# First pages of three experts loaded ahead of the page table, with page buffers in memory of their own

## The chip, the cores and the metric

The kernel runs on one core of a Trainium2 chip. The metric is the device time in microseconds of one execution, the median of several timed runs. Beside it there is one profiled execution, whose page and trace are quoted below. The engines are called as in the profile: PE is the matmul engine, PEld its weight loads, DVE the vector engine, ACT the scalar engine, POOL the general engine, which here issues the indexed transfers, and SP the engine that issues most plain transfers.

## The reference

Two layers work on 128 graphs of 64 nodes with 256 features, 8192 rows in all. Layer 0 is a graph stage and a mixture over 64 experts, layer 1 a graph stage and a mixture over 8 experts. Only the end of layer 1 matters for the change (cut):

```python
# --- layer 1 ---
x = x + _L1_gnn_ref(_layernorm(x), adj, ...)          # the graph stage
x = x + _L1_ffn_ref(_layernorm(x), ...)

def _L1_ffn_ref(x, Wg, bg, bias, W1, b1, W2, b2):     # 8 experts, 256 -> 512 -> 256
    x_flat = x.reshape(-1, D_MODEL)
    gate_logits = x_flat @ Wg + bg + bias
    topk_vals, topk_idx = jax.lax.top_k(gate_logits, 2)
    topk_w = jax.nn.softmax(topk_vals, axis=-1)
    combine = (jax.nn.one_hot(topk_idx, 8) * topk_w[..., None]).sum(axis=1)
    h = jax.nn.relu(jnp.einsum('td,edh->teh', x_flat, W1) + b1)
    y = jnp.einsum('teh,ehd->ted', h, W2) + b2
    return jnp.einsum('ted,te->td', y, combine).reshape(x.shape)
```

Each row goes to 2 of 8 experts, and which ones is known only when its logits are.

## The kernel before

It has four large stages, one after the other: layer 0's graph stage in 32 blocks of 256 rows, layer 0's experts, a block stage (the end of layer 0, layer 1's graph stage and its routing, again 32 blocks), and layer 1's experts. In the block stage each normalized row is scattered, with its two routing values, into a table in main memory that has a region per expert. For that the kernel keeps the running end of each region (`run`), counts a block's rows per expert on PE, works out the places on DVE, and sends the rows with four indexed transfers from POOL:

```python
# in class Router
    def places(self, b, hot):
        # ... the places of the block's rows from the counts in PSUM and the running ends ...

    def send(self, row, xs):
        for t in range(self.T):
            for k in range(self.K):
                i = self.nc.gpsimd.indirect_dma_start(
                    out=self.table[:, :], out_offset=bass.IndirectOffsetOnAxis(ap=row[:, t, k:k + 1], axis=0),
                    in_=xs[:, t, k, :], in_offset=None)
                self.alone(i.ins, "send")

    def fill(self, engine, row):
        i = engine.dma_start(
            out=self.table[ds(row, self.pg), :].rearrange("(t p) d -> p t d", p=P),
            in_=self.filler)
        self.alone(i.ins, "fill", "send", "full")
```

`alone` tells the framework which transfers touch different rows, so that they need not wait for each other. When all blocks are sent, `page_table` turns the counts into pages of 256 rows: first the full pages of all experts, then the partial ones. It leaves, for each page, its first row in the table and its expert (`tab`), which engines read into registers:

```python
        v.tensor_scalar(full, cnt, 1.0 / pg, (pg - 1.0) / (2 * pg), op0=ALU.mult, op1=ALU.subtract)
        v.tensor_scalar(full, full, MAGIC, None, op0=ALU.add)
        v.tensor_scalar(full, full, -MAGIC, None, op0=ALU.add)
        v.scalar_tensor_tensor(part, full, -float(pg), cnt, op0=ALU.mult, op1=ALU.add)
        v.tensor_scalar(part, part, 0.0, None, op0=ALU.is_gt)
        v.tensor_tensor_scan(cum, num, self.zero, 0.0, op0=ALU.add, op1=ALU.add)
        # ... start row and expert of each page into self.tab ...

    def load(self, what, i, engine):

        top = (self.spare, self.E - 1)[what]
        _, v = self.nc.values_load_multi_w_load_instructions(
            self.tab[i // 4:i // 4 + 1, what, :], engines=[engine], min_val=0, max_val=top,
            skip_runtime_bounds_check_because="the page table holds no other values for any counts")
        return v
# ...
    def fetch(self, i, row, out):
        d = self.nc.sync.dma_start(out=out, in_=self.table[ds(row, self.pg), :].rearrange("(t p) d -> p t d", p=P))
        if i < self.full_pages:
            self.tc.declare_no_dep(d.ins, group=self.name + "fill", reason="full pages have no filler rows")
            self.tc.add_to_no_dep_group(self.name + "full", d.ins)
```

The stages of a block or page are staggered: the pairs are a lag and a function, and the order of the pairs is the order of each engine's instructions for PE, DVE and ACT, which is kept as written. The order on the queues of SP and POOL is the framework's.

```python
        def place1(b):
            B = blocks[b]
            r1.send(r1.places(b, B["hot"]), B["xs"])

        staggered(NB, (
            (-2, load3),
            # ...
            (3, choose1),
            # ...
            (3, count1),
            # ...
            (3, place1),
            (0, layer_out_c),
            (4, load_w2),
        ))
        r1.page_table(work.tile([P, 512], F32, name="scratch", bufs=1))

    with tc.tile_pool(name="wx1", bufs=2) as wx, \
            tc.tile_pool(name="pt4", bufs=2, space=PSUM) as pt_pool, \
            tc.tile_pool(name="ph4", bufs=4, space=PSUM) as ph_pool, \
            tc.tile_pool(name="py4", bufs=2, space=PSUM) as py_pool:
        PG = 2 * P
        pages = [dict() for _ in range(r1.pages)]
        regs = {}

        def fetch1(i):
            Q = pages[i]
            if i % 4 == 0 or i == r1.likely_pages:
                regs["row"], regs["esp"] = r1.load(0, i, ENG.SP), r1.load(1, i, ENG.SP)
            row, e = regs["row"][i % 4], regs["esp"][i % 4]
            Q["x"] = x = wx.tile([P, 2, W], F32, name="px", bufs=4)
            r1.fetch(i, row, x)
            Q["w"] = w = wx.tile([P, F1W], F32, name="pw", bufs=3)
            nc.sync.dma_start(out=w, in_=fw1[ds(e, 1)].rearrange("o p f -> p (o f)"))
            Q["b2"] = b2 = wx.tile([P, D], F32, name="pb2", bufs=4)
            nc.sync.dma_start(out=b2, in_=a["L1_ffn_b2"][ds(e, 1), :].to_broadcast([P, D]))

        def flip1(i):
            Q = pages[i]
            pt = pt_pool.tile([P, KD, PG], F32, name="pt")
            ops.transpose(pt, Q["x"])
            Q["xT"] = xT = wx.tile([P, KD, PG], F32, name="pxT")
            nc.scalar.copy(xT, pt)

        # up(i): 16 products with Q["w"], relu on ACT
        # down(i): 16 products with fw2[expert], bias and weight on DVE, two adding scatters from POOL

        stages = (-2, fetch1), (0, flip1), (1, down), (0, up)
        staggered(r1.likely_pages, stages)
        with tc.If(r1.needed(r1.likely_pages)):
            staggered(r1.pages, stages, r1.likely_pages)
```

`likely_pages` is 69 here; pages beyond that run only if the routing needs them. The page pool `wx` is opened after the pools of the block stage are closed, so its buffers lie where the block stage's tiles lay. A constant row that is added by a matmul is split into bf16 parts, and stored twice side by side, by `row_parts`:

```python
    def row_parts(rest, name):

        part = small.tile([P, D], BF16, name="part", bufs=1)
        out = const.tile([P, 2, D], BF16, name="p_" + name)
        for i in range(3):
            nc.vector.tensor_copy(part, rest)
            nc.vector.tensor_sub(rest, rest, part)
            if i == 0:
                nc.vector.tensor_scalar(out[:, 0, :], part, ident[:, 0:1], None, op0=ALU.mult)
            else:
                nc.vector.scalar_tensor_tensor(out[:, 0, :], part, ident[:, i:i + 1], out[:, 0, :],
                                               op0=ALU.mult, op1=ALU.add)
        nc.vector.tensor_copy(out[:, 1, :], out[:, 0, :])
        return out

```

Of the kernel before, what the change touches and what calls it, by code (L numbers as in the profile page):

```python
# [78 lines left out]
class Router:  # L79
# [15 lines left out]
    def __init__(self, tc, pool, small, dram, n, D, E, K, T, pg, S, epoch, name, total=None):  # L95
# [46 lines left out]
        self.table = dram.tile([self.spare + pg, self.W], F32, name=name + "x")  # L142
        self.fill(nc.sync, self.spare)

# [21 lines left out]
    def fill(self, engine, row):  # L166
        i = engine.dma_start(
            out=self.table[ds(row, self.pg), :].rearrange("(t p) d -> p t d", p=P),
            in_=self.filler)
        self.alone(i.ins, "fill", "send", "full")  # L170
# [113 lines left out]
    def send(self, row, xs):  # L284
        for t in range(self.T):
            for k in range(self.K):
                i = self.nc.gpsimd.indirect_dma_start(  # L287
                    out=self.table[:, :], out_offset=bass.IndirectOffsetOnAxis(ap=row[:, t, k:k + 1], axis=0),
                    in_=xs[:, t, k, :], in_offset=None)
                self.alone(i.ins, "send")  # L290
# [18 lines left out]
    def page_table(self, scratch):  # L309
# [29 lines left out]
        v.tensor_scalar(part, part, 0.0, None, op0=ALU.is_gt)  # L339
        v.tensor_tensor_scan(cum, num, self.zero, 0.0, op0=ALU.add, op1=ALU.add)  # L340
# [48 lines left out]
    def needed(self, n):  # L389

        _, (v,) = self.nc.values_load_multi_w_load_instructions(
            self.total_pages[0:1, :], min_val=0, max_val=self.pages,
            skip_runtime_bounds_check_because="these pages hold any routing")
        return v > n

# [16 lines left out]
def two_layer_gnn_moe_kernel(ctx: ExitStack, tc: tile.TileContext, a: dict, out: bass.AP):  # L412
# [49 lines left out]
    def row_parts(rest, name):  # L462

        part = small.tile([P, D], BF16, name="part", bufs=1)
        out = const.tile([P, 2, D], BF16, name="p_" + name)
        for i in range(3):
            nc.vector.tensor_copy(part, rest)
            nc.vector.tensor_sub(rest, rest, part)
            if i == 0:
                nc.vector.tensor_scalar(out[:, 0, :], part, ident[:, 0:1], None, op0=ALU.mult)  # L470
            else:
                nc.vector.scalar_tensor_tensor(out[:, 0, :], part, ident[:, i:i + 1], out[:, 0, :],
                                               op0=ALU.mult, op1=ALU.add)
        nc.vector.tensor_copy(out[:, 1, :], out[:, 0, :])
        return out
# [316 lines left out]
    fw2 = keep.tile([P, E1, KF, D], F32, name="fw2")  # L792
    with tc.tile_pool(name="c3", bufs=1) as c3, \
# [18 lines left out]
        pg = pmix.tile([P, T, E1], F32, name="pg")  # L812
        r1.begin(counts, work, pmix.tile([P, 2, T, E1], F32, name="pos"))
# [154 lines left out]
        def place1(b):  # L968
            B = blocks[b]
            r1.send(r1.places(b, B["hot"]), B["xs"])  # L970

# [24 lines left out]
    with tc.tile_pool(name="wx1", bufs=2) as wx, \  # L996
            tc.tile_pool(name="pt4", bufs=2, space=PSUM) as pt_pool, \
# [3 lines left out]
        pages = [dict() for _ in range(r1.pages)]  # L1001
        regs = {}

        def fetch1(i):
            Q = pages[i]
            if i % 4 == 0 or i == r1.likely_pages:
                regs["row"], regs["esp"] = r1.load(0, i, ENG.SP), r1.load(1, i, ENG.SP)
            row, e = regs["row"][i % 4], regs["esp"][i % 4]
            Q["x"] = x = wx.tile([P, 2, W], F32, name="px", bufs=4)
            r1.fetch(i, row, x)  # L1010
# [3 lines left out]
            nc.sync.dma_start(out=b2, in_=a["L1_ffn_b2"][ds(e, 1), :].to_broadcast([P, D]))  # L1014

# [18 lines left out]
        def down(i):  # L1034
            Q = pages[i]
            if i < E1:
                r1.fill_end(i)
            if i % 4 == 0 or i == r1.likely_pages:
                regs["e"] = r1.load(1, i, ENG.PE)

# [6 lines left out]
            for t in range(2):  # L1047
                for c in range(KF):
                    nc.tensor.matmul(py[:, t, :], lhsT=Q["hid"][:, c, ts(t, P)],  # L1049
                                     rhs=fw2[:, ds(regs["e"][i % 4], 1), c, :].rearrange("p o d -> p (o d)"),  # L1050
# [7 lines left out]
        staggered(r1.likely_pages, stages)  # L1058
        with tc.If(r1.needed(r1.likely_pages)):
            staggered(r1.pages, stages, r1.likely_pages)  # L1060
# [32 lines left out]
```

## Time and profile before

| what | value |
|---|---|
| timed runs | 2144.85 us median of 3 (2144.35 to 2147.32) |
| span of the profiled execution | 2446.3 us |
| PE, PEld busy | 2036.7 us (83%), 1744.9 us (71%) |
| DVE, ACT, POOL busy | 1186.3 us (48%), 1013.6 us (41%), 1157.1 us (47%) |
| moved by transfers | 398.93 MB, mean 163 GB/s |
| mean granted PE clock | 0.931 |

The profiled execution is longer than a timed one, so a length in the trace is not yet a length in the metric. The page cuts the span into 40 slices of 61 us. Each digit is the busy share of a slice in tenths, and PEclk is the clock granted to PE in tenths of full speed:

```profile
PE   7888888888884578877878886888888699999998
DVE  5777776776666322222222234777777222222221
POOL 0464555455355566666666661333333344444444
PEclk9999989988896799989999998999999799999999
DMA  3233433343236677655555537877773476676665
```

The layer 0 stages take the first 24 digits, the block stage about the next seven, where DVE's digits are 7, and layer 1's experts the rest, where PE's are 9. Between the last two stages there is a slice with a 6 for PE and a 7 for its clock.

### The profile page before, as it was taken

The page shows a single profiled execution, that of the slowest core. Times are in us where ns is not written, and L with a number is a line of the kernel's source. Part 1 is how long each engine was busy: PE and PEld are TensorE (multiplying, and loading weights), DVE is VectorE, ACT ScalarE, POOL GpSimd, SP SyncE. Part 2 cuts the span into 40 slices and gives each one's busy share as a digit, 9 for nine tenths or more (in the row PEclk, how much of TensorE's full clock was granted, in tenths as well). Part 3 has the DMA queues.
Part 4 walks back from the last instruction along what each step waited for, and adds up shares of the span by engine and source line. Part 5 has one row for each costly group of instructions (what it writes and reads, how often), then busy time and mean ns, then how long its engine had stood idle before and what let it go on. Part 6 is the DMA issues. An engine that isn't in the chain of part 4 may idle for free.

```text
span 2446.3 us, 37355 instructions
## 1 busy us (share of the span) xinstructions
PE 2036.7 (83%) x10564; PEld 1744.9 (71%) x10564; DVE 1186.3 (48%) x3952; ACT 1013.6 (41%) x2037; POOL 1157.1 (47%) x1146
## 2 busy tenths in 40 slices
PE   7888888888884578877878886888888699999998
PEld 6776766767673467766666665777777588888887
DVE  5777776776666322222222234777777222222221
ACT  5766665665662112111111113555555233333332
POOL 0464555455355566666666661333333344444444
PEclk9999989988896799989999998999999799999999
DMA  3233433343236677655555537877773476676665
GB/s 100 90 119 97 132 122 128 123 131 126 88 101 195 199 222 223 203 171 171 178 176 171 146 87 253 300 233 240 232 228 128 141 177 163 156 169 162 161 162 119
DMA packets 284092, 398.93 MB, mean 163 GB/s; under 512 B 56536, under 2 KB 237928, under 8 KB 283888
## 3 DMA queue, kind: packets, MB, share of 16 engines
q1 hardware_dynamic: 204032, 247.67, 34.7%
q0 software_dynamic: 64800, 136.14, 18.7%
q10 hardware_dynamic: 15056, 12.69, 1.6%
q8 instruction: 93, 1.52, 0.3%
q14 instruction: 111, 0.91, 0.1%
HBM read 223.89 MB, written 177.69 MB: 164 GB/s over the span
## 4 chain that ended last, share of the span: by engine, by line
PE 58%; DVE 10%; issue 9%; another core or an unknown queue 8%; ACT 8%; DMA 3%; POOL 2%; SPq 1%; ACTq 0%; POOLq 0%; DVEq 0%
PE py L770 10%; PE ph L1030 9%; PE py L1049 9%; PE ph L599 4%; PE ps L833 3%; PE ps L632 3%; PE pt L755 3%; PE po L844 2%; PE pz L905 2%; PE pc L916 2%; ACT xs L651 2%; ACT lat L602 2%; DVE lat L621 2%; PE ps L76 2%
## 5 line engine op out<-in xcount | busy, mean ns | idle before, releaser
L287 POOL DMA_INDIRECT r0x<-xs,r0row x384 | 390.2, 1016 | 421.0 <-issue 307.1
L770 PE MATMUL py<-lat,pxT 128*128 x1696 | 443.4, 408 | 122.2 <-ACT pxT L757 82.3
L294 POOL DMA_INDIRECT r0y<-py_s,px x424 | 412.5, 973 | 245.9 <-DVE py_s L775 109.9
L770 PEld LDWEIGHTS py<-lat,pxT 128*128 128x128 f32 x1696 | 328.4, 204 | 179.5 <-ACT pxT L757 94.3
L775 DVE TENSOR_SCALAR py_s<-py,px 128x256 f32<-128x256 f32 x424 | 179.5, 478 | 480.0 <-PE py L770 137.8
L302 POOL DMA_INDIRECT out_x<-py_s,px x138 | 214.1, 1551 | 310.1 <-DVE p L1044 124.9
L757 ACT COPY pxT<-pt 128x512 f32<-128x512 f32 x212 | 119.1, 589 | 556.8 <-remote 182.4
L632 PE MATMUL ps<-lat 128*128 128x256 f32 x1024 | 275.7, 420 | 8.3 <-issue 8.0
L1032 ACT ACTIVATE phid<-ph,pw 128x256 f32<-128x256 f32 x276 | 131.0, 475 | 323.8 <-issue 217.4
L632 PEld LDWEIGHTS ps<-lat 128*128 128x128 f32 x1024 | 217.9, 216 | 49.2 <-issue 13.1
L1030 PE MATMUL ph<-pxT,pw 128*128 128x256 f32 x1104 | 252.3, 382 | 0.8 <-ACT pxT L1021 0.8
L1049 PE MATMUL py<-fw,phid 128*128 x1104 | 249.7, 379 | 0.0
L599 PE MATMUL ph<-lat 128*128 128x256 f32 x1024 | 232.8, 386 | 6.8 <-DVE lat L621 6.1
L287 POOL DMA_INDIRECT r1x<-xs,r1row x128 | 126.5, 988 | 226.4 <-DVE bn_rs L881 135.7
L1030 PEld LDWEIGHTS ph<-pxT,pw 128*128 128x128 f32 x1104 | 211.6, 192 | 30.4 <-ACT pxT L1021 1.2
L1049 PEld LDWEIGHTS py<-fw,phid 128*128 128x128 f32 x1104 | 204.5, 190 | 25.0
L599 PEld LDWEIGHTS ph<-lat 128*128 128x128 f32 x1024 | 195.4, 193 | 34.3 <-DVE lat L621 4.8
L755 PE MATMUL pt<-ident,px 128*128 128x128 f32 x848 | 136.3, 285 | 35.4 <-DMA px<-r0x 33.3
L755 PEld LDWEIGHTS pt<-ident,px 128*128 128x128 f32 x848 | 112.5, 148 | 61.9 <-issue 40.5
L602 ACT ACTIVATE lat<-ph,c_L_gnn_b 128x256 f32<-128x256 f32 x256 | 103.9, 470 | 123.4 <-PE ph L599 48.4
L1043 DVE TENSOR_SCALAR p<-p 128x2 f32<-128x2 f32 x69 | 11.9, 173 | 242.3 <-ACT p L1042 238.9
L1052 DVE TENSOR_TENSOR py_s<-py,pb 128x512 f32<-128x512 f32 x69 | 47.7, 692 | 155.6 <-PE py L1049 155.5
(265 smaller groups left out, 2894.5 us busy)
## 6 DMA issues: line engine op xcount, KB each, us to landing
px<-r0x SPq DMA_DIRECT2D x424, 129.0 KB
y<-r0y SPq DMA_DIRECT2D x64, 768.0 KB
pw<-in_L_ffn_W1b SPq DMA_DIRECT2D x69, 514.0 KB
px<-r1x SPq DMA_DIRECT2D x69, 258.0 KB
x<-x SPq DMA_DIRECT2D x64, 256.0 KB
pb<-in_L_ffn_b SPq DMA_DIRECT2D x69, 128.0 KB
r0x<-r0filler ACTq DMA_DIRECT2D x64, 129.0 KB
lat<-in_x SPq DMA_DIRECT2D x32, 256.0 KB
```

The costliest lines, as they stand in the source:

```text
L287: i = self.nc.gpsimd.indirect_dma_start(out=self.table[:, :], out_offset=bass.IndirectOffsetOnAxis(ap=row[:, t, k:k + 1], axis=0), in_=xs[ ...
L294: i = self.nc.gpsimd.indirect_dma_start(out=self.answer[:, :], out_offset=bass.IndirectOffsetOnAxis(ap=x[:, self.D:self.D + 1].bitcast(I32 ...
L302: i, d = f"{self.name}add{i}", self.nc.gpsimd.indirect_dma_start(out=self.total[:, :], out_offset=bass.IndirectOffsetOnAxis(ap=x[:, self.D ...
L599: nc.tensor.matmul(ph[:, c, :], lhsT=w1[:, k, ts(2 * j + c, P)], rhs=B["aggT"][:, k, :], start=(k == 0), stop=(k == KD - 1))
L602: nc.scalar.activation(sq[:, 2 * j + c, :], ph[:, c, :], AF.Square, bias=b1[:, 2 * j + c:2 * j + c + 1], scale=1.0)
L632: nc.tensor.matmul(B["po"][:, t, :], lhsT=B["hT"][:, c, ts(t, P)], rhs=w2[:, c, :], start=False, stop=(t == T - 1 and c == KH - 1))
L755: nc.tensor.transpose(pt[:, k, ts(q, P)], Q["px", q][:, 0, ts(k, P)], ident)
L770: nc.tensor.matmul(py[:, q, :], lhsT=Q["xT"][:, k, ts(q, P)], rhs=lat[:, ds(regs["e"][(2 * j + q) % 4], 1), k, :].rearrange("p o d -> p (o ...
L775: nc.vector.tensor_scalar(y[:, q, :], py[:, q, :], px[:, 0, D + 1:D + 2], None, op0=ALU.mult)
L1030: nc.tensor.matmul(ph, lhsT=w[:, k * F1 + c * P:k * F1 + (c + 1) * P], rhs=Q["xT"][:, k, :], start=(k == 0), stop=(k == KD - 1))
L1032: nc.scalar.activation(hid[:, c, :], ph, AF.Relu, bias=w[:, KD * F1 + c:KD * F1 + c + 1], scale=1.0)
L1049: nc.tensor.matmul(py[:, t, :], lhsT=Q["hid"][:, c, ts(t, P)], rhs=fw2[:, ds(regs["e"][i % 4], 1), c, :].rearrange("p o d -> p (o d)"), st ...
```

## The change

Layer 1's first page of experts 0, 1 and 2 need not wait for the page table: their rows start at a known place, and once 256 rows of an expert are sent, its first page is complete. After block 16 of 32 the kernel looks which of the three have their first page full (`look`) and leaves in `firsts` the row of that page, or the row of a page of zeros. The rows of later blocks form a group of their own ("late"), for which these pages need not wait. The three pages are run ahead of the others, as pages -3 to -1, and the page table leaves them out (`taken`), so that 66 pages from the table follow. Their expert is known when the program is built, so their products with W2 need no register. For their buffers to be filled while the block stage still runs, the page pool is opened before the pools of that stage and so lies in memory of its own. To make room, `row_parts` stores its row once and hands out an access that reads it twice.

The whole diff:

```diff
--- before.py
+++ after.py
@@ -140,7 +140,23 @@
             nc.gpsimd.iota(fill_to, pattern=[[P, pg // P]], base=n, channel_multiplier=1)
             nc.sync.dma_start(out=total[n:n + pg, :].rearrange("(t p) d -> p t d", p=P), in_=self.filler[:, :, :D])
         self.table = dram.tile([self.spare + pg, self.W], F32, name=name + "x")
+        self.taken = None
         self.fill(nc.sync, self.spare)
+
+    def look(self, m):
+
+        v = self.nc.vector
+        self.taken = self.pool.tile([P, self.E], F32, name=self.name + "taken")
+        self.firsts = self.pool.tile([P, 4], I32, name=self.name + "firsts")
+        t = self.small.tile([P, m], F32, name=self.name + "look")
+        v.memset(self.taken, 0.0)
+        v.tensor_sub(t, self.run[:, 0, :m], self.base[:, :m])
+        v.tensor_scalar(self.taken[:, :m], t, float(self.pg), None, op0=ALU.is_ge)
+        v.tensor_scalar(t, self.base[:, :m], float(self.spare), None, op0=ALU.subtract)
+        v.tensor_mul(t, t, self.taken[:, :m])
+        v.memset(self.firsts, 0.0)
+        v.tensor_scalar(self.firsts[:, :m], t, float(self.spare), None, op0=ALU.add)
+        self.full_pages -= m
 
     def iota(self, shape, pattern, m, name):
         t = self.pool.tile(shape, F32, name=self.name + name)
@@ -167,7 +183,7 @@
         i = engine.dma_start(
             out=self.table[ds(row, self.pg), :].rearrange("(t p) d -> p t d", p=P),
             in_=self.filler)
-        self.alone(i.ins, "fill", "send", "full")
+        self.alone(i.ins, "fill", "send", "late", "full")
 
     def choose(self, logits):
 
@@ -282,12 +298,13 @@
         return out
 
     def send(self, row, xs):
+        groups = ("send", "late") if self.taken is None else ("late", "send")
         for t in range(self.T):
             for k in range(self.K):
                 i = self.nc.gpsimd.indirect_dma_start(
                     out=self.table[:, :], out_offset=bass.IndirectOffsetOnAxis(ap=row[:, t, k:k + 1], axis=0),
                     in_=xs[:, t, k, :], in_offset=None)
-                self.alone(i.ins, "send")
+                self.alone(i.ins, *groups)
 
     def reply(self, x, y):
 
@@ -337,6 +354,11 @@
         v.tensor_scalar(full, full, -MAGIC, None, op0=ALU.add)
         v.scalar_tensor_tensor(part, full, -float(pg), cnt, op0=ALU.mult, op1=ALU.add)
         v.tensor_scalar(part, part, 0.0, None, op0=ALU.is_gt)
+        if self.taken is not None:
+            assert J == 1
+            v.tensor_sub(full, full, self.taken)
+            v.scalar_tensor_tensor(self.map[:, 0, :], self.taken, float(pg), self.map[:, 0, :],
+                                   op0=ALU.mult, op1=ALU.add)
         v.tensor_tensor_scan(cum, num, self.zero, 0.0, op0=ALU.add, op1=ALU.add)
         self.total_pages = self.pool.tile([P, 1], I32, name=n + "total")
         v.tensor_copy(self.total_pages, cum[:, V - 1:V])
@@ -393,6 +415,17 @@
             skip_runtime_bounds_check_because="these pages hold any routing")
         return v > n
 
+    def load_first(self, engine):
+        _, v = self.nc.values_load_multi_w_load_instructions(
+            self.firsts[0:1, :], engines=[engine], min_val=0, max_val=self.spare,
+            skip_runtime_bounds_check_because="a first page, or that of zeros")
+        return v
+
+    def fetch_first(self, row, out):
+
+        d = self.nc.sync.dma_start(out=out, in_=self.table[ds(row, self.pg), :].rearrange("(t p) d -> p t d", p=P))
+        self.tc.declare_no_dep(d.ins, group=self.name + "late", reason="full pages get no rows")
+
     def fetch(self, i, row, out):
         d = self.nc.sync.dma_start(out=out, in_=self.table[ds(row, self.pg), :].rearrange("(t p) d -> p t d", p=P))
         if i < self.full_pages:
@@ -462,17 +495,15 @@
     def row_parts(rest, name):
 
         part = small.tile([P, D], BF16, name="part", bufs=1)
-        out = const.tile([P, 2, D], BF16, name="p_" + name)
+        out = const.tile([P, D], BF16, name="p_" + name)
         for i in range(3):
             nc.vector.tensor_copy(part, rest)
             nc.vector.tensor_sub(rest, rest, part)
             if i == 0:
-                nc.vector.tensor_scalar(out[:, 0, :], part, ident[:, 0:1], None, op0=ALU.mult)
+                nc.vector.tensor_scalar(out, part, ident[:, 0:1], None, op0=ALU.mult)
             else:
-                nc.vector.scalar_tensor_tensor(out[:, 0, :], part, ident[:, i:i + 1], out[:, 0, :],
-                                               op0=ALU.mult, op1=ALU.add)
-        nc.vector.tensor_copy(out[:, 1, :], out[:, 0, :])
-        return out
+                nc.vector.scalar_tensor_tensor(out, part, ident[:, i:i + 1], out, op0=ALU.mult, op1=ALU.add)
+        return out.unsqueeze(1).to_broadcast([P, 2, D])
 
     def by_tile(ap):
         return ap.rearrange("(t p) d -> p t d", p=P)
@@ -790,6 +821,7 @@
     fw1 = a["L1_ffn_W1b1"]
     F1W = fw1.shape[2]
     fw2 = keep.tile([P, E1, KF, D], F32, name="fw2")
+    wx = ctx.enter_context(tc.tile_pool(name="wx1", bufs=2))
     with tc.tile_pool(name="c3", bufs=1) as c3, \
             tc.tile_pool(name="work3", bufs=2) as work, \
             tc.tile_pool(name="ps3", bufs=3, space=PSUM) as psum, \
@@ -810,6 +842,7 @@
         nc.gpsimd.memset(one, 1.0)
         blocks = [dict() for _ in range(NB)]
         pg = pmix.tile([P, T, E1], F32, name="pg")
+        FIRST = 3
         r1.begin(counts, work, pmix.tile([P, 2, T, E1], F32, name="pos"))
 
         def load3(b):
@@ -968,6 +1001,8 @@
         def place1(b):
             B = blocks[b]
             r1.send(r1.places(b, B["hot"]), B["xs"])
+            if b == NB // 2:
+                r1.look(FIRST)
 
         staggered(NB, (
             (-2, load3),
@@ -993,25 +1028,35 @@
         r1.page_table(work.tile([P, 512], F32, name="scratch", bufs=1))
 
 
-    with tc.tile_pool(name="wx1", bufs=2) as wx, \
-            tc.tile_pool(name="pt4", bufs=2, space=PSUM) as pt_pool, \
+    with tc.tile_pool(name="pt4", bufs=2, space=PSUM) as pt_pool, \
             tc.tile_pool(name="ph4", bufs=4, space=PSUM) as ph_pool, \
             tc.tile_pool(name="py4", bufs=2, space=PSUM) as py_pool:
         PG = 2 * P
-        pages = [dict() for _ in range(r1.pages)]
+        pages = {i: dict() for i in range(-FIRST, r1.pages)}
         regs = {}
 
-        def fetch1(i):
+        likely = r1.likely_pages - FIRST
+
+        def load1(i, e):
             Q = pages[i]
-            if i % 4 == 0 or i == r1.likely_pages:
-                regs["row"], regs["esp"] = r1.load(0, i, ENG.SP), r1.load(1, i, ENG.SP)
-            row, e = regs["row"][i % 4], regs["esp"][i % 4]
-            Q["x"] = x = wx.tile([P, 2, W], F32, name="px", bufs=4)
-            r1.fetch(i, row, x)
             Q["w"] = w = wx.tile([P, F1W], F32, name="pw", bufs=3)
             nc.sync.dma_start(out=w, in_=fw1[ds(e, 1)].rearrange("o p f -> p (o f)"))
             Q["b2"] = b2 = wx.tile([P, D], F32, name="pb2", bufs=4)
             nc.sync.dma_start(out=b2, in_=a["L1_ffn_b2"][ds(e, 1), :].to_broadcast([P, D]))
+
+        def fetch1(i):
+            Q = pages[i]
+            Q["x"] = x = wx.tile([P, 2, W], F32, name="px", bufs=4)
+            if i < 0:
+                if i == -FIRST:
+                    regs["first"] = r1.load_first(ENG.SP)
+                r1.fetch_first(regs["first"][i + FIRST], x)
+                load1(i, i + FIRST)
+                return
+            if i % 4 == 0 or i == likely:
+                regs["row"], regs["esp"] = r1.load(0, i, ENG.SP), r1.load(1, i, ENG.SP)
+            r1.fetch(i, regs["row"][i % 4], x)
+            load1(i, regs["esp"][i % 4])
 
         def flip1(i):
             Q = pages[i]
@@ -1033,10 +1078,11 @@
 
         def down(i):
             Q = pages[i]
-            if i < E1:
+            if 0 <= i < E1:
                 r1.fill_end(i)
-            if i % 4 == 0 or i == r1.likely_pages:
+            if i >= 0 and (i % 4 == 0 or i == likely):
                 regs["e"] = r1.load(1, i, ENG.PE)
+            e = regs["e"][i % 4] if i >= 0 else i + FIRST
 
             p = wx.tile([P, 2], F32, name="p")
             nc.scalar.activation(p, Q["x"][:, :, D + 1], AF.Exp)
@@ -1047,7 +1093,7 @@
             for t in range(2):
                 for c in range(KF):
                     nc.tensor.matmul(py[:, t, :], lhsT=Q["hid"][:, c, ts(t, P)],
-                                     rhs=fw2[:, ds(regs["e"][i % 4], 1), c, :].rearrange("p o d -> p (o d)"),
+                                     rhs=fw2[:, ds(e, 1), c, :].rearrange("p o d -> p (o d)"),
                                      start=(c == 0), stop=(c == KF - 1))
             nc.vector.tensor_add(y, py, Q["b2"].unsqueeze(1).to_broadcast([P, 2, D]))
             for t in range(2):
@@ -1055,9 +1101,9 @@
                 r1.add(i, Q["x"][:, t, :], y[:, t, :])
 
         stages = (-2, fetch1), (0, flip1), (1, down), (0, up)
-        staggered(r1.likely_pages, stages)
-        with tc.If(r1.needed(r1.likely_pages)):
-            staggered(r1.pages, stages, r1.likely_pages)
+        staggered(likely, stages, -FIRST)
+        with tc.If(r1.needed(likely)):
+            staggered(r1.pages, stages, likely)
 
 
 def kernel(**inputs):
```

## The prediction

> **What bounds the kernel now.** I read the table of busy time by stage first, because the page's averages (PE 83%, DVE 48%) mix several stages with different limits. Its columns are the stretch, its length, the busy time and instructions of PE, PE's weight loads, DVE, ACT and POOL, then granted clock, DMA share and GB/s.
>
> ```profile
> 1484.00:1912.00 428.00, 372.72 (x2368) 322.24 (x2368) 320.18 (x1407) 226.48 (x481) 129.53 (x153) 0.97 0.68 228
> 1912.00:1926.00 14.00, 1.09 (x5) 0.72 (x5) 5.02 (x34) 0.59 (x1) 3.90 (x4) 0.50 0.33 101
> 1926.00:2410.00 484.00, 484.00 (x2360) 425.94 (x2361) 109.70 (x325) 171.88 (x395) 198.54 (x128) 0.99 0.69 166
> ```
>
> The third row is layer 1's expert stage: PE busy 484 of 484 us, so it is bound by PE and nothing that only loads faster can shorten it. The first row is the block stage before it, PE 87% busy. Between them lies a hole of 14 us in which PE does 1.09 us of work. The timeline of PE shows its two edges (start, duration, what, idle before it):
>
> ```profile
> 1907.82 1.88 PE L951 MATMUL pg<-m_L_ffn_Wg,xn3T 128*128 128x8 f32 x8 [0.73 <-ACT xn3T L945]
> 1911.39 0.20 PE L191 MATMUL pos<-r1hot,r1tri 128*128 128x16 bf16 x2 [1.70 <-DVE r1which L181]
> 1911.45 0.20 PE L191 MATMUL pos<-r1hot,r1ones 128*128 128x16 bf16 x2
> 1924.11 1.09 PE L76 MATMUL pt<-ident,px 128*128 128x128 f32 x4 [12.46 <-DMA px<-r1x]
> 1925.99 6.35 PE L1030 MATMUL ph<-pxT,pw 128*128 128x256 f32 x16 [0.80 <-ACT pxT L1021]
> 1932.61 3.62 PE L1049 MATMUL py<-fw,phid 128*128 x16
> 1936.07 3.62 PE L1030 MATMUL ph<-pxT,pw 128*128 128x256 f32 x16
> ```
>
> The count of the last block ends at 1911.65; the first page's transposes start 12.46 us later. The chain of waits says what fills the hole (cut to its corners):
>
> ```profile
> 1912.61 0.17 DVE r1row L281
> ...
> 1917.49 2.56 DMA r1x<-xs,r1row
> ...
> 1920.57 0.40 SPq L397
> ...
> 1921.54 3.69 DMA pw<-in_L_ffn_W1b
> 1925.24 0.04 issue
> ```
>
> So: DVE computes the last rows and meanwhile the page table (ready at 1917.74), POOL issues four scatters, the last of them lands at 1920.05, SP loads registers and issues, and page and weights land at about 1924 and 1925.2. All of it is serial, and it happens once.
>
> **What the Trainium skill says.** "DMA: Bandwidth & Descriptors", section "Rules for kernel authors": issue the DMA early, compute, and wait late, so that its fixed cost overlaps. That is the change in one sentence; the trace has the cost it means (2.56 us for a scatter, 3.69 us for the weights, nothing beside them). "TensorE: Matmul & The Clock Gate", section "Part 1: The HAM clock gate": an idle PE falls to half rate and needs some 3.4 us of work to come back. The trace agrees: the first sixteen products after the hole take 6.35 us, the next sixteen 3.62 us by the timeline (3.45 us apart in the chain). I found no page on how a profiled execution differs from a timed one in the middle of a kernel, which matters below.
>
> **The change part by part.**
>
> *Removed from the path.* PE's order in the changed program is: count of block 31, then at once the transposes of the first early page, its first products, transposes of the second, second products of the first, and so on. The early page's rows, weights and bias are issued long before: in SP's order the weights stand among the loads of blocks 11 to 14, right behind the eight W2 loads, and the rows among those of block 23, after block 16 was sent. The first transposes have no wait left but one for an older matmul of PE's own. So they start near 1911.7 instead of 1924.11: **12.4 us**. The step after (copy, 0.80 us of idle) stays. I give nothing for the clock: PE is already at half rate at 1907.82 (1.88 us for eight gate products that take 1.06 us in the steady blocks) and waits 1.70 us after that, so the first products will again be slow, about 6 us.
>
> *Whether three pages are enough.* In the changed run the early pages occupy PE from 1911.7: 1.1 + 0.8 + 6.35 us to the end of the first products, 1919.9, then two periods of 7.35 us (0.44 + 3.46 + 3.45 in the chain) to 1934.6, when the transposes of the first table page are due. That page cannot be issued before the last scatter lands (1920.05) and is there 3.5 us after its issue at 1920.57, so 10 us early. Its weights need one of three buffers, the first early page's, free at 1919.9: no wait. The next page's rows need the first of four row buffers, free when the first early page's additions have landed. In the kernel before, those additions are issued at 1938.22 and 1940.15 and the buffer's next load at 1944.55, which is 20.4 us after that page's transposes. Shifted: 1932.1, landed at about 1935.6, due 1934.6 + 7.35 = 1942. Enough.
>
> *Added.* Seven small DVE instructions once, in block 16's placement. Neighbours of that kind take 0.16 to 0.19 us and start about 0.2 us apart: 1.4 us. In a steady block (12.7 us) DVE idles 1.19 us for the gate product and 0.75 us for ACT, and the normalized rows which stand behind the new instructions are finished on ACT at 1713.80 and used by PE at 1716.43: 2.6 us of room. Cost 0 to 0.5 us. Two more instructions in the page table (0.4 us) are no longer on the path.
>
> *Moved.* Three loads each of 258, 514 and 128 KB, 2.7 MB, go into the block stage. The total of pages stays: 69 before, 3 + 66 after. I counted the routing of these inputs from the reference: 61 full and 8 partial pages, 69; and after 17 blocks experts 0, 1 and 2 hold 1264, 997 and 738 rows, so all three first pages of 256 are full and none of the early pages is one of zeros. The conditional tail isn't entered either way.
>
> *Removed elsewhere.* Three bf16 copies of 0.226 us in the first stage, 0.7 us of DVE, in part on the path: 0 to 0.5 us. The matmuls that read the copy now read the same row twice, 128x512 as before.
>
> Sum in the trace: 12.4 - 0.3 + 0.2 = about 12.3 us of 2446.3.
>
> **From trace to timed runs.** The profiled execution lasted 2446 us, timed ones 2145. If all of it shrank alike, 12.3 us would be 10.8. But the stages on either side of the hole have full clock and a busy PE, so I suspect the difference sits in the first and third stage, and then the hole is nearly as long in a timed run. I choose 11.8 us: 2144.85 - 11.8 = **2133 us**, a ratio of 1.0055.
>
> **The rivals.**
>
> 1. *The early loads disturb the block stage.* For: while W2 is loaded (512 KB per block) the DMA share is 0.89 at 295 GB/s against 0.72 at 235 afterwards, and the weights of the early pages stretch just this period by three blocks. Against: with the extra load the blocks take 12.7 us, and without it 12.7 us; PE waits there for ACT's copy, not for DMA. If those three blocks slowed as far as the bytes go, 2.7 MB at 235 GB/s is 11.5 us, and the gain is gone: 2144. I give this 5%, and 15% to a loss of 2 to 4 us.
> 2. *A new wait takes the hole's place.* The first table page could come late, because SP's queue, in order, holds its row load behind a buffer. The numbers above leave 6 to 10 us; a late page would show as an idle PE before the fourth or fifth transposes, and cost at most the rest of the hole, so 2136 to 2140.
> 3. *The moved memory costs elsewhere.* With the page buffers in memory of their own the block stage's tiles lie on other old tiles, and its first load, copy and transposes carry waits on nearly every queue. Against: the first load there already waits for the last reply of the stage before (PE idles 17.28 us for it), and the new waits are for work no later than that. Cost 0, at worst 1 us.
> 4. *More than the hole.* If PE keeps its clock over the seam, the first products take 3.5 instead of 6.35 us: 2.9 us more, 2130.
>
> **Range and chances.** The centre is 2133; rival 4 sets the lower end, half the gain lost the upper. The timed runs before spread by 3 us, which adds about 1 us on each side: 2128 to 2139. Two per cent are 43 us, more than three times the hole, so faster by that much is next to impossible: 0.01. Slower by that much would need a stall that repeats in every block or page, of which the order shows none: 0.02. Within: 0.97.
>
> **What will show it.** Right: PE's first page transposes follow the last count within 1 us, the first products still take about 6 us, no idle of PE before the transposes of the fourth and fifth page, a row load for the first table page at its old time near 1920, and the expert stage as long as before. Wrong: blocks 11 to 24 longer than 12.7 us (rival 1), a DMA named as releaser before a later page (rival 2), or a longer wait than 17.28 us at the start of the block stage (rival 3).

## The result, and the profile after

| | before | changed |
|---|---|---|
| timed runs, median | 2144.6 us (4 runs, 2143.31 to 2147.32) | 2134.84 us (4 runs, 2134.48 to 2135.26) |
| span of the profiled execution | 2446.3 us | 2133.3 us |
| PE busy | 2036.7 us (83%) | 1939.7 us (91%) |
| moved by transfers | 398.93 MB | 398.96 MB |

The ratio of the times is 0.9953, interval 0.9936 to 0.997: 9.8 us less. A second comparison gave 0.996 (0.9948 to 0.9973): 2138.26 us against 2148.48.

Neither the two spans nor the two busy times can be subtracted: the first profiled execution of the kernel before was drawn out, for a reason that isn't known, as were four more further below, while a second trace of the same kernel has a span of 2148.6 us, with PE busy for 1938.8. Stage lengths are compared with that one. The eight traces with spans of 2131 to 2150 us are called the short traces below.

The table of busy time by stage, changed kernel: the block stage after its first wait, the 14 us after the last count, the expert stage. The columns are as in the prediction.

```profile
1220.00:1609.00 389.00, 372.26 (x2370) 322.48 (x2371) 318.87 (x1412) 229.41 (x481) 132.59 (x153) 0.97 0.77 258
1609.00:1623.00 14.00, 13.27 (x56) 11.10 (x55) 7.17 (x41) 5.92 (x11) 5.53 (x5) 0.81 0.36 111
1623.00:2107.00 484.00, 483.88 (x2372) 425.96 (x2371) 111.67 (x330) 170.77 (x396) 202.89 (x131) 1.00 0.69 164
```

The middle one of these stretches in the kernel before, from its second trace:

```profile
1610.00:1624.00 14.00, 1.09 (x4) 0.72 (x4) 4.96 (x34) 0.58 (x1) 3.89 (x4) 0.50 0.36 102
```

Read the two 14 us rows against each other: PE's busy time goes from 1.09 to 13.27 us, while DVE still does its page table (4.96 us before, within 7.17 now) and POOL its scatters. The expert stage's row stands as before: PE busy all the time.

The timeline of PE at the seam, changed kernel (start, duration, what, and the idle time before it with what ended it):

```profile
1602.63 0.48 PE L76 MATMUL ps<-ident,xs 128*128 128x128 f32 x1 [3.43 <-ACT xs L971]
...
1604.97 1.88 PE L984 MATMUL pg<-m_L_ffn_Wg,xn3T 128*128 128x8 f32 x8 [0.73 <-ACT xn3T L978]
1608.54 0.20 PE L207 MATMUL pos<-r1hot,r1tri 128*128 128x16 bf16 x2 [1.69 <-DVE r1hot L199]
1608.59 0.20 PE L207 MATMUL pos<-r1hot,r1ones 128*128 128x16 bf16 x2
1608.64 1.09 PE L76 MATMUL pt<-ident,px 128*128 128x128 f32 x4
1610.47 5.56 PE L1075 MATMUL ph<-pxT,pw 128*128 128x256 f32 x16 [0.73 <-ACT pxT L1066]
...
1616.30 3.62 PE L1095 MATMUL py<-fw,phid 128*128 128x256 f32 x16
...
1630.56 0.60 PE L76 MATMUL pt<-ident,px 128*128 128x128 f32 x4
```

The first page's transposes have no wait; the one idle time left is 0.73 us for ACT's copy. The line at 1630.56 is the fourth set of transposes, the first page from the table, and it has no idle time before it either. For the rest of the expert stage the list of PE's waits is empty.

The transfers of the early pages, as SP issues them (weights of the first early page, its rows, the rows of the first table page; the two other early pages follow the first within 28 us):

```profile
1320.33 0.46 SPq L1043 DMA_DIRECT2D pw<-in_L_ffn_W1b  x1
...
1454.95 0.39 SPq L426 DMA_DIRECT2D px<-r1x  x1
...
1617.10 0.39 SPq L430 DMA_DIRECT2D px<-r1x  x1
```

The early rows are issued 154 us before PE needs them. The first table page's rows are issued at 1617.10, 8.3 us after the last count (8.8 us in the kernel before, 1618.39 after a count that ended at 1609.61), and used at 1630.56.

### The profile page after: what moved, and what is told of

The parts are those of the page before. It is cut to its first block, busy times and chain, and to the rows that moved or that the text cites. A ratio compares the mean times of both kernels' runs of the same rounds, so it can differ in the third digit from the quotient of the medians.

```text
span 2133.3 us, 37321 instructions
## 1 busy us (share of the span) xinstructions
PE 1939.7 (91%) x10564; PEld 1682.9 (79%) x10564; DVE 1185.1 (56%) x3958; ACT 1019.3 (48%) x2037; POOL 1164.4 (55%) x1146
## 2 busy tenths in 40 slices
DMA packets 284094, 398.96 MB, mean 187 GB/s; under 512 B 56536, under 2 KB 237928, under 8 KB 283888
## 5 line engine op out<-in xcount | busy, mean ns | idle before, releaser
L304 POOL DMA_INDIRECT r0x<-xs,r0row x384 | 395.4, 1030 | 256.6 <-issue 171.8
L801 PE MATMUL py<-lat,pxT 128*128 x1696 | 411.2, 386 | 38.2 <-DVE py_s L806 21.5
L806 DVE TENSOR_SCALAR py_s<-py,px 128x256 f32<-128x256 f32 x424 | 185.6, 480 | 361.1 <-PE py L801 164.6
L801 PEld LDWEIGHTS py<-lat,pxT 128*128 128x128 f32 x1696 | 307.3, 191 | 89.4 <-issue 29.1
L1095 PE MATMUL py<-fw,phid 128*128 (+1 forms) x1104 | 249.8, 379 | 0.1
L663 PE MATMUL ps<-lat 128*128 128x256 f32 x1024 | 237.9, 381 | 0.0
L663 PEld LDWEIGHTS ps<-lat 128*128 128x128 f32 x1024 | 193.4, 191 | 24.7
L786 PE MATMUL pt<-ident,px 128*128 128x128 f32 x848 | 128.3, 275 | 35.6 <-DMA px<-r0x 35.6
L786 PEld LDWEIGHTS pt<-ident,px 128*128 128x128 f32 x848 | 106.7, 142 | 57.8 <-issue 36.3
L866 PE MATMUL ps<-ident,y 128*128 128x128 f32 x768 | 93.0, 278 | 37.2 <-DMA r1x<-r1filler 35.6
```

Source lines behind the costliest of these rows:

```text
L304: i = self.nc.gpsimd.indirect_dma_start(out=self.table[:, :], out_offset=bass.IndirectOffsetOnAxis(ap=row[:, t, k:k + 1], axis=0), in_=xs[ ...
L663: nc.tensor.matmul(B["po"][:, t, :], lhsT=B["hT"][:, c, ts(t, P)], rhs=w2[:, c, :], start=False, stop=(t == T - 1 and c == KH - 1))
L786: nc.tensor.transpose(pt[:, k, ts(q, P)], Q["px", q][:, 0, ts(k, P)], ident)
L801: nc.tensor.matmul(py[:, q, :], lhsT=Q["xT"][:, k, ts(q, P)], rhs=lat[:, ds(regs["e"][(2 * j + q) % 4], 1), k, :].rearrange("p o d -> p (o ...
L806: nc.vector.tensor_scalar(y[:, q, :], py[:, q, :], px[:, 0, D + 1:D + 2], None, op0=ALU.mult)
```

## The experiments

**How many pages, which part of the change.** Four kernels were timed together, on a chip where the kernel before took 2149.91 us (median of 51 runs). The first two shorten the set of early pages:

```diff
-        FIRST = 3
+        FIRST = 1        # first1; FIRST = 2 in first2
```

One early page, expected:

> One early page instead of three (68 from the table). The hole theory (PE idle at the seam is all that changes, layout and early loads are free): the early page has its transposes and first products, about 7.2 us, in a hole of 12.5, and PE then waits about 5 us more for the first table page; gain about 4 us of 2145, 2141. If layout and early loads take back a fixed 2 to 3 us: gain 1 to 2 us, 2143. PE idle before the first table page's transposes: about 5 us.

Measured: 2144.69 us, ratio 0.9971 (0.9961 to 0.998): 5.2 us gained by the medians and 6.2 by the ratio, where 4 were expected. Its timeline of PE has the rest of the old wait behind the first page, whose own work needs no wait:

```profile
1625.00 0.66 PE L76 MATMUL pt<-ident,px 128*128 128x128 f32 x4 [4.08 <-DMA px<-r1x]
1625.50 5.31 PE L1095 MATMUL py<-fw,phid 128*128 128x256 f32 x16
```

and its chain of waits names what the second page, now the first from the table, still waits for (start, duration, what):

```profile
1618.38 0.97 POOL r1x L304
...
1619.65 2.44 DMA r1x<-xs,r1row
...
1622.11 2.85 DMA px<-r1x
```

This is the old chain, scatter then row load, of which one page's work covers the first part. The page that follows costs more than its 4.08 us of idle time, since its second products run slow again: 5.31 us instead of 3.62.

Two early pages, expected:

> Two early pages. Hole theory: two pages cover 14.8 us from the last count to the first table page's transposes, more than the 12.5 us the table page needs, so the same gain as three pages, within 1 us (2133 to 2136). If the early loads cost the block stage in proportion to their bytes: about 1 us faster than three pages. If two pages are too few: idle PE before the first table page, slower than three by that idle.

Measured: 2138.47 us, ratio 0.9948 (0.9928 to 0.9968), the same gain as with three. PE has no idle time before the first table page. Two pages are enough; the third is reserve.

Next, the memory without the early pages. `FIRST` is 0 and the look after block 16 is left out, so all pages come from the table, but the page pool lies in memory of its own and the row of `row_parts` is stored once:

```diff
-        FIRST = 3
+        FIRST = 0
...
-            if b == NB // 2:
-                r1.look(FIRST)
```

> No early page: only the page buffers in memory of their own and the row stored once. Hole theory: nothing, 2143 to 2147, hole at the seam still 12.5 us. If the moved memory makes the block stage start later or slows it: 2 to 3 us slower than before, 2147 to 2148.

Measured: 2147.94 us, ratio 0.9992 (0.9983 to 1.0001). The hole is there as before, 11.15 us and then 2.15 us for the weights:

```profile
1622.97 1.09 PE L76 MATMUL pt<-ident,px 128*128 128x128 f32 x4 [11.15 <-DMA px<-r1x]
1626.21 6.08 PE L1073 MATMUL ph<-pxT,pw 128*128 128x256 f32 x16 [2.15 <-DMA pw<-in_L_ffn_W1b]
```

And the early pages without the memory: three of them, but the pool is opened behind the block stage, as before.

```diff
-    wx = ctx.enter_context(tc.tile_pool(name="wx1", bufs=2))
...
-    with tc.tile_pool(name="pt4", bufs=2, space=PSUM) as pt_pool, \
+    with tc.tile_pool(name="wx1", bufs=2) as wx, \
+            tc.tile_pool(name="pt4", bufs=2, space=PSUM) as pt_pool, \
```

> Three early pages, but the page buffers in the block stage's memory again, as before. Hole theory: the buffers are free only when the last rows are scattered, so the early loads start at the old time, and only the page table's place in the chain is saved, which was done 2 us before the scatter landed anyway: gain 0 to 1 us, hole at the seam about 12 us. If the early look at the counts alone gave the gain: about 10 us faster.

Measured: 2151.13 us, ratio 1.0007 (0.9995 to 1.0019): nothing gained. PE at the seam:

```profile
1624.09 1.09 PE L76 MATMUL pt<-ident,px 128*128 128x128 f32 x4 [13.00 <-DMA px<-r1x]
```

and SP, whose early row loads have a known address since the look, but go out only now:

```profile
1620.02 0.40 SPq L426 DMA_DIRECT2D px<-r1x  x1
```

In the changed kernel the same load goes out at 1454.95. So neither part does anything alone: knowing the rows early is worth nothing while their buffer belongs to the stage before, and the free buffer is worth nothing while the rows are unknown.

**The kernels again, and a version that goes further.** On another chip, where the kernel before took 2148.48 us (median of 11 runs). The kernel before, for a second trace:

> The kernel before, unchanged, for a second trace: the first trace lasted 2446 us where timed runs take 2145, that of the changed kernel 2133. If the first trace was drawn out at the seam too: a hole of about 11.2 us, as in the run with the layout alone, a span near 2145 and blocks of 11.3 us. If the hole was right and something else takes 2 to 3 us back: a hole of 12.5 us, and some other stage shorter than after's by 2 to 3 us.

Measured: 2150.37 us in one execution, span 2148.6. The hole has its old length, and behind it PE waits 1.45 us, for the weights, where the first trace had 0.80 us for ACT's copy:

```profile
1609.41 0.20 PE L191 MATMUL pos<-r1hot,r1ones 128*128 128x16 bf16 x2
1622.09 1.09 PE L76 MATMUL pt<-ident,px 128*128 128x128 f32 x4 [12.48 <-DMA px<-r1x]
1624.63 6.31 PE L1030 MATMUL ph<-pxT,pw 128*128 128x256 f32 x16 [1.45 <-DMA pw<-in_L_ffn_W1b]
...
1631.21 3.62 PE L1049 MATMUL py<-fw,phid 128*128 x16
```

So the hole in the first trace was right, as in the second expectation. The other stage that goes with it, shorter than the changed kernel's by 2 to 3 us, isn't found (below, in the comparison with the prediction).

The changed kernel again:

> The changed kernel, with more rounds, for the ratio. Hole theory with a hole of 11.2 us, 0.1 us of copy wait and up to 0.8 us of slow clock saved: 11 to 12 us faster than before, ratio 0.9944 to 0.9949. If 2 to 3 us are taken back elsewhere: 8 to 9 us, ratio 0.9958 to 0.9963.

Measured: 2138.26 us, ratio 0.996 (0.9948 to 0.9973), 10.2 us gained by the medians; span 2136.4. This lies between the two expectations and decides for neither.

The last two blocks leave PE idle while each waits for DVE and ACT (3.43, 0.73 and 1.69 us in the lines above). The version `seam_fill` puts early work there: the first page's transposes stand before the count of block 30, its sixteen first products behind it, the second page's transposes behind the last gate products. The fetches of the early pages move into the block stage in the program, too, and the scatters are told that they need not wait for them.

```diff
+            if b == NB // 2 + 2:
+                for i in range(-FIRST, 0):
+                    fetch1(i)
... (in the list of the block stage)
+            (3, first_loads),
...
+            (3, at(NB - 2, early_up, -3)),
+            (3, at(NB - 2, early_relu, -3, 0)),
...
+            (2, at(NB - 1, early_relu, -3, 1, 2)),
...
+            (2, at(NB - 1, early_relu, -3, 3)),
...
+            (2, at(NB - 2, early_flip, -3)),
+            (2, at(NB - 1, early_flip, -2)),
... (the expert stage leaves out what was done)
-        stages = (-2, fetch1), (0, flip1), (1, down), (0, up)
+        stages = (-2, rest(fetch1, 0)), (0, rest(flip1, -1)), (1, down), (0, rest(up, -2))
```

> A version of the changed kernel that puts parts of the early pages into PE's remaining waits of the last two blocks: the first early page's transposes ahead of the count of block 30, its sixteen first products between that count and block 31's transposes, where PE waits 3.4 us, and the second page's transposes after the last gate product. If PE's waits at the seam are free room: 0.4 + 3.5 + 0.4 us of work moved into them, 0.7 us of wait for the first copy gone, and a clock that stays up, which takes 2 us off the first products and 0.8 us off the last gate product: 7 to 8 us faster than the changed kernel, ratio to before 0.991 to 0.992. If the last blocks' chain of ACT and DVE is delayed by what is put in: 2 to 4 us.

Measured: 2133.24 us, ratio 0.9931 (0.9917 to 0.9945): 15.2 us less than before by the medians, some 5 us less than the changed kernel beside it, and the best of all versions. Its timeline of PE:

```profile
1601.74 5.39 PE L1054 MATMUL ps<-pxT,pw 128*128 128x256 f32 x16
...
1609.15 1.06 PE L1012 MATMUL pg<-m_L_ffn_Wg,xn3T 128*128 128x8 f32 x8 [0.73 <-ACT xn3T L1006]
...
1612.65 5.24 PE L1135 MATMUL py<-fw,phid 128*128 128x256 f32 x16 [0.63 <-DVE r1place L286]
```

The first products fill the gap that was 3.43 us, and the last gate products are at full speed (1.06 instead of 1.88 us). But two groups of sixteen still run partly slow, 5.39 and 5.24 us instead of 3.62: 3.4 us lost in the two, against 1.9 us in the changed kernel's one slow group. So the clock takes 1.5 us more than in the changed kernel, where the expectation had it give 2 us back on the first products. That is a shortfall of some 3.4 us, enough for the 2 to 3 us that are missing from the 7 to 8 expected. The table of busy time shows the clock (third column from the right) fall while PE is at work:

```profile
1600.00:1601.60 1.60, 0.46 (x4) 0.29 (x4) 1.41 (x9) 0.58 (x1) 1.09 (x2) 1.00 0.23 83
1601.60:1603.00 1.40, 1.36 (x8) 1.15 (x8) 1.33 (x5) 0.00 (x0) 0.97 (x1) 0.69 0.26 94
1603.00:1605.00 2.00, 2.00 (x6) 1.53 (x6) 0.66 (x3) 0.00 (x0) 0.00 (x0) 0.50 0.57 197
1605.00:1607.00 2.00, 2.00 (x9) 1.50 (x7) 1.01 (x7) 1.36 (x3) 0.00 (x0) 0.86 0.00 0
```

During the idle time (first row) it is still 1.00, and it is 0.50 in the third, where PE is busy throughout.

**Where the rest of the gain is.** In the short traces the time from the last count to the end is 538.99 us before and 524.51 and 522.86 us in the changed kernel, some 15 us less, while the timed runs gain 10. Two more profiled executions of either kernel were to tell whether something is paid back ahead of the seam. For the kernel before:

> The kernel before again, for the length of its stages alone. If the seam's gain (about 14 us in the traces) is partly paid back ahead of the seam, the last count of the block stage ends some 3 us earlier here than in the changed kernel (near 1609 against 1612 us), in every pair. If it is only spread, the ends overlap.

> As the first look at the kernel before: last count near 1609 us if something is paid back ahead of the seam, overlapping with the changed kernel's if it is spread.

and for the changed kernel:

> The changed kernel again. Paid back ahead of the seam: last count near 1612 us or later, 3 us after that of the kernel before. Only spread: within the range of the kernel before. From the last count to the end 523 to 525 us by either theory, against 537 to 539.

> As the first look at the changed kernel: last count near 1612 us or later if something is paid back ahead of the seam, overlapping with that of the kernel before if it is spread.

Measured: 2477.28 and 2486.61 us before, 2473.78 and 2464.74 us after. All four were drawn out like the first profiled execution, so the absolute times written down don't apply to them. The last count ends at 1936.5 and 1948.4 us before, at 1944.5 and 1938.5 us after: the ranges overlap, but with 12 us between two executions of one kernel a difference of 3 us can't be read from them. The question stays open. What can be compared is the part behind the last count:

| last count to the end, us | | | | | mean |
|---|---|---|---|---|---|
| before: first trace, second, two more | 534.65 | 538.99 | 539.02 | 536.42 | 537.3 |
| changed: first trace, second, two more | 524.51 | 522.86 | 527.49 | 524.49 | 524.8 |

The difference of the means is 12.4 us, but it mixes unlike executions (the single values spread by 4 to 5 us): among the short traces it is some 15 us, among the drawn-out ones (three before, two changed) 10.7. PE's timeline gives a narrower measure, from the end of the last count to the start of the first page's second products (`py`): 20.96, 21.60, 20.33 and 20.83 us before, 7.51, 7.42, 7.75 and 7.52 us in the changed kernel. The seam itself is 13.4 us shorter.

## Why the prediction was right, step by step

**The hole: right, and the seam gave a little more.** Removed were 12.4 us of serial waiting in the prediction. The transposes follow the last count at once (0 instead of 12.46 us), and with `layout_only` and `shared_mem` the hole is back. The seam as a whole is 13.4 us shorter, because of two small terms that the prediction set to zero. (That the means of the table above differ by just 12.4 us is luck, given what they mix.) The wait behind the copy is 0.73 instead of 0.8 to 1.45 us, since the weights no longer come last; and the first sixteen products take 5.56, 5.47, 5.79 and 5.57 us in the changed kernel's traces against 6.35, 6.31, 5.53 and 6.37 us before, half a microsecond less on average. The 3.69 us that the prediction gave the weights' load, as a case of a transfer's fixed cost, are not fixed: in the second trace the same load takes 5.13.

**"The first products will again be slow": right.** About 6 us were predicted, 5.47 to 5.79 measured. Rival 4, in which PE keeps its clock, would have needed 3.5 us. They are no faster without a hole: in `shared_mem`, behind 13.00 us of idle time, they take 5.33 us. The hole wasn't what made PE slow: the gate products of the last block, before it, already took 1.88 us, after 3.43 us of idle time. The Trainium skill, "TensorE: Matmul & The Clock Gate", "Part 1: The HAM clock gate", lets the clock fall after an idle window of about 3.4 us. The trace agrees only in part, for the clock falls before the 3.43 us gap is over (table of busy time, changed kernel):

```profile
1597.00:1600.00 3.00, 0.69 (x8) 0.52 (x8) 2.30 (x13) 0.00 (x0) 2.18 (x3) 1.00 0.24 88
1600.00:1602.60 2.60, 0.00 (x0) 0.00 (x0) 2.00 (x12) 1.13 (x3) 0.00 (x0) 0.61 0.45 152
```

A mean of 0.61 in the second row means 1.00 for its first 0.6 us and 0.50 from then on. The gap began at 1599.20, so the clock fell some 1.4 us into it. In the 3 us before 1600 PE had worked for only 0.69. With that gap filled, in `seam_fill`, the gate products take 1.06 us. More on this in the last section.

**"Three pages are enough": right, with one to spare.** Ten microseconds of slack were worked out for the first table page. Its rows were issued at 1617.10 and used at 1630.56; at the 3.5 us that the prediction took for the load, that is 10 us. The run with two pages shows no wait, the run with one page waits 4.08 us. Each page covers about 7.35 us, so the second was needed and the third wasn't.

**Rival 1, the early loads disturb the block stage: refuted.** From one block's large products to those of the next it is 11.29 or 11.30 us in every steady block of all eight short traces, with and without early loads. PE is the bound there, so a slower transfer would show only if PE had to wait for it. Two stretches of the changed kernel's stage table, with W2 and the early weights, and with the look and the early rows:

```profile
1300.00:1402.00 102.00, 102.00 (x669) 89.42 (x668) 89.55 (x400) 64.21 (x135) 38.34 (x45) 1.00 0.90 297
1402.00:1515.00 113.00, 113.00 (x742) 99.02 (x742) 100.13 (x450) 71.35 (x150) 43.79 (x51) 1.00 0.83 271
```

PE is busy for all of both, at a DMA share of 0.90 as at 0.83. The prediction's evidence for this step was off, though: its 12.7 us per block, with a wait for ACT's copy in each, belong to the first trace. Ten blocks there (1700 to 1827 us) have 13.8 us of that wait, and the same blocks of the second trace none.

**The added and removed DVE work: no cost seen.** The seven instructions of the look run from 1451.05 to 1452.02, in the second of these stretches; 0 to 0.5 us had been given, and the block's period doesn't show it. What the three removed copies in the first stage are worth can't be told from these runs.

**Rival 2, a new wait takes the hole's place: refuted** for two and three pages by the empty list of PE's waits behind the seam; it is what happens with one.

**Rival 3, the moved memory: a small part of it exists, and no loss is shown.** The prediction named a wait longer than 17.28 us at the start of the block stage as its sign. That number too was of the first trace. Compared with the second, the wait for the first mixture is a little longer with memory of its own. The kernel before, from its second trace, and then the changed one:

```profile
1218.11 5.74 PE L833 MATMUL ps<-ident,y 128*128 128x128 f32 x24 [34.33 <-DMA y<-r0y]
```

```profile
1219.91 5.49 PE L866 MATMUL ps<-ident,y 128*128 128x128 f32 x24 [35.58 <-DMA r1x<-r1filler]
```

In all six short traces with the pool in memory of its own it is 35.5 to 35.6 us, in the two with shared memory 34.2 to 34.3, and the releaser changes: now a transfer of filler rows (`r1x<-r1filler`, in two of the six `out_x<-r1filler`). But that the stage as a whole gets longer isn't seen: its first large products start 60.5 to 63.8 us after PE's last work in the stage before, in any order, and the kernel with the memory alone is not slower (0.9992, interval 0.9983 to 1.0001). "Cost 0, at worst 1 us" is not contradicted, but a loss of about 1 us can't be excluded either.

**From trace to timed runs: the right idea, but some 1.8 us too much gain; this is the term that was mis-sized.** The prediction suspected that the extra 300 us of its trace lay ahead of the hole, and scaled 12.3 us down only to 11.8. The traces bear that out: up to the last work before the block stage the first trace takes 1466.8 us and the second 1183.8, which is 283.0 of the 297.7 us between the spans, and the block stage gives another 19.1 (444.9 against 425.8), while the part behind the last count is not longer. Yet the timed runs give 9.8 and 10.2 us, not the 11.8 that were chosen, let alone the 13.4 by which the seam is shorter. The miss is 1.8 us of 2133.0 predicted, and 12.4 us would be a ratio of 0.9942, inside the intervals of both the first comparison and the run with two pages, but below that of the second comparison (0.9948 to 0.9973). Whether the rest is given back ahead of the seam stays open: no stage in the traces is longer by 2 us in all versions with early pages, and the start of the block stage alone varies by 3 us between executions. One candidate is the 1.3 us of rival 3: from PE's last work before the block stage to the last count it takes 424.5 to 427.5 us (mean 426.7) in the six short traces with memory of its own, and 425.8 and 424.2 in the two with shared memory. The ranges overlap, and the timed runs with the memory alone speak against it.

## What to carry to other kernels

Where a stage ends in a table that only its last piece of data completes, look for work of the next stage that an earlier prefix already fixes; as much of it as the chain takes (here 12.5 us, two pages of 7.35) is enough. It needs both the early knowledge and a buffer that the old stage doesn't own: a prefetch into recycled memory goes out when that stage is done, however early its address is known (at 1620.02 instead of 1454.95 us here). And before a length is read off a trace, compare the trace's span with the timed runs: when it is longer, find out in which stages. Here the hole, behind the stages that were drawn out, could be read as it stood: 12.46 us in the long trace, 12.48 in the short one.

## What was unexpected of the hardware

PE's clock can fall in the work behind a gap, and no gap of 3.4 us is needed for it. In `seam_fill` only 1.18 us of idle time stand ahead of the first products, and PE was busy for 8 us before; still the clock drops to 0.50 within them. With one early page the 4.08 us of idle time pass at a clock of 1.00, and the slow part is in the work behind them (table of busy time, `first1`):

```profile
1621.00:1625.00 4.00, 0.00 (x0) 0.00 (x0) 0.00 (x0) 0.44 (x1) 0.00 (x0) 1.00 0.45 118
1625.00:1627.00 2.00, 2.00 (x9) 1.71 (x10) 0.00 (x0) 1.28 (x2) 0.00 (x0) 0.70 0.96 271
1627.00:1629.00 2.00, 2.00 (x6) 1.59 (x5) 0.33 (x2) 0.79 (x2) 0.00 (x0) 0.50 0.97 282
1629.00:1631.00 2.00, 2.00 (x10) 1.76 (x9) 0.16 (x1) 0.00 (x0) 0.00 (x0) 0.94 0.89 281
```

From the mean clocks of the rows, with 1.00 and 0.50 as the only values, the slow stretch lasts from 1625.8 to 1629.2 us here and from 1602.1 to 1605.6 in `seam_fill`: 3.4 us in both.

So a gap costs more than its length: here the sixteen products behind it take 5.31 us instead of 3.62, 1.7 us on top of 4.08. The clock seems to answer to how busy PE was in the few microseconds before, and a short stretch with little work seems to be enough to lower it; how little wasn't measured. The busy share alone doesn't settle it: in `seam_fill` PE worked for 2.16 of the 3.42 us from 1585.07 on, and the clock stayed at 1.00 behind them, and for 2.23 of the 3.41 us from 1598.73 on, and it fell.
